# A cross-attention block on one core: one operand of the MLP made elsewhere, x scaled by another engine, and sums and stores reordered

## The chip, the cores and the metric

One core of a Trainium2 chip runs one program. The metric is the time of one execution in microseconds (us), as the device reports it; lower is better. Engines are named as in the profile: PE (TensorE, matmuls and transposes), DVE (VectorE), ACT (ScalarE), POOL (GpSimd) and SP (SyncE, which here does nothing but issue DMAs). Each engine runs its own instructions in the order in which the kernel emits them, and waits for the others by semaphores.

## What is computed

A cross-attention layer with an MLP in float32. `x` and `ctx` have 8 batches of 256 tokens of width 512 each. Cut to what matters:

```python
x = layer_norm(hidden_states, ln1_w, ln1_b)
q = x @ q_w + q_b                      # 512 x 512, 16 heads of 32
k, v = ctx @ k_w + k_b, ctx @ v_w + v_b
attn = softmax(where(mask, q @ k.T / sqrt(32), lowest))
hidden = (attn @ v) @ cproj_w + cproj_b + hidden_states
y = layer_norm(hidden, ln2_w, ln2_b)
y = gelu(y @ fc_w + fc_b)              # 512 -> 2048
return hidden + y @ proj_w + proj_b    # 2048 -> 512
```

## The kernel before

**Tiling.** The 2048 rows of tokens are worked on in 4 groups of 512 (`NG = 4`, `G = 512`), each two batches of 256. A tile has 128 partitions. First comes the attention of all four groups, then the MLP of all four.

**Strassen products.** Every 512-wide matrix product is made of seven products of quarters instead of eight, after Strassen and Winograd. Each needs sums and differences of the quarters of both operands: `A_SUMS` for a weight (s3 = 11 - 21, s2 = 22 - s3, 21 = s2 + 11, s4 = 12 - s2), `B_SUMS` for the tokens. An operand therefore has seven blocks: four quarters, one of them overwritten, and three sums. These sums run on POOL and DVE beside PE. In the attention's projections `strassen` (L417) emits the seven products as pieces p0 to p6.

**The attention's order is written by hand.** A group has 8 units (`u`), two per head group. The loop at L1040 emits, for unit n: the scores of unit n+2, softmax pieces of n+2 (DVE takes the maximum, ACT the exponential), the transposes of unit n's probabilities (`turn_probs`, L688, four per unit, PSUM tag "pt" with two buffers), the division of unit n+1 (`divide`, L676, four operations on POOL), and `attend` (L700), whose result is copied from a "pt" buffer to the tile `att` by ACT at L716. Between these steps other work is hung in: `between[g, u, 0..1]` holds PE's pieces of the next group's projections, `aside[g, u, 0..3]` holds sums, loads and stores. `begin(g, u, i, f)` appends to `aside[g, u, i]`; `spread` does so for a list. So a place such as (0, 6, 1) reads: group 0, unit 6, second stop.

**Layer norm of x.** `layer_norm` (L236) returns three kinds of pieces: statistics on DVE, the roots on POOL (L250 and L251), and the scaling of a 128 x 512 tile (L254) on a given engine. In the attention `norm_over` (L770) hangs these into units 2 to 4 for group g+2's x, with POOL as the engine of the scaling. The transposes of x (`turn_x`, L397, PE at L267) follow in units 5 and 6.

**The lent buffer.** The MLP's weight `fc_w` is also needed as Strassen sums. They are made during the attention and kept in DRAM (`w2_dram`). In group 0 this uses a place of the weights, `fc["a"]`, and a buffer lent by the attention: `fc["b"]`, which lies in the tile "att" that group 1 will need (L996). `sums` and `split` (L895 and L900) put each sum at its place; `keep_s3`, `keep_own` and `keep_first_s2` store results on SP. Before L716 may write group 1's first `att`, everything that reads the lent buffer has to be done, its stores included.

**The end of the attention.** `project_out(3)` (L618) projects the last group; its results are added on POOL to the residual `res` (L623) and stored from there to `hid_dram` (L624). `bias_res(3)` (L613, L616) adds a bias to one quarter of the residual on POOL and is emitted before the products 21, 22 and 12 of the projection. After the stores comes `load_w2("c")` (L1077).

**The MLP.** For each group `product(k, ...)` (L1232) makes the seven products of `fc_w`'s operands with the tokens, and `FC_ORDER` gives each its operand. An operand `w2[g, k]` occupies one of the places "q", "k", "c" and "v", and the end of a product loads another operand into the place that it frees (L1292). Within a product there are seven parts on PE: `sub(1)`, `sub(6)`, `sub(7)`, `sub(5)`, and then a second part into banks 1, 7 and 5. ACT copies bank 1 to u1 (L1270) after the first part, and the second part into bank 1 accumulates after that copy. DVE makes u2 and u3 and moves results to one of four slots of `h["s3"]`, from which POOL adds them to `h` (`made`, L1254). When an `h` is complete, `gelu` queues eight ACTIVATEs (L1214), which `some_gelus` lets out between ACT's copies, in program order.

Product 6 of group 0 is a special case: its operand, quarter 22 of `fc_w`, is loaded raw after product 3 (into place "q"), its four sums run on POOL after product 4's adds (L1307 and L1308), and the sums are stored for the later groups (L1309).

After the products the second Strassen product follows, with `proj_w` in `pw` (seven tiles of 128 x 8 x 256: four quarters and t1, t2, t4). Its sums of `pw` are made in group 0 by DVE, 16 pieces let out by `some_pw` (L1316 and on): in order 12, t2, t1, t4. Its sums of `h` run on POOL (`sum_h`: s3, s2, s1, s4).

Of the kernel before, what the change touches and what calls it, by code (L numbers as in the profile page):

```python
# [10 lines left out]
F32 = mybir.dt.float32  # L11
U8 = mybir.dt.uint8
AF = mybir.ActivationFunctionType
# [3 lines left out]
P = 128  # L17
# [5 lines left out]
def tile_xattn_block(  # L23
# [164 lines left out]
    def load_w2(at):  # L188

        if not w2_order:  # L190
            return
        g, k = w2_order.pop(0)
        t = rows_of(place(f"w2_{g}_{k}", at).t)
        n = FC_ORDER[k][0]
        if (g, k) == (0, 6):
            load_fc_quarter(lambda i: t[:, i], n)
        elif n in OWN:
            load_fc_quarter(lambda i: t[:, i], n, (0, 1, 3))
            nc.sync.dma_start(t[:, 2], w2_dram[QI[n]][:, 2])
            nc.sync.dma_start(t[:, 4:7], w2_dram[QI[n]][:, 4:7])  # L200
        else:
            nc.sync.dma_start(t, w2_dram[QI[n]])
        w2[g, k], w2_place[g, k] = t, at
# [32 lines left out]
    def layer_norm(tiles, tag, eng=nc.vector):  # L236


        mv = small.tile([P, NT, 2], F32, tag="mv", name=f"mv_{tag}")
        rstd = small.tile([P, NT], F32, tag="rstd", name=f"rstd_{tag}")  # L240
        layer_norm.last = mv, rstd

        def stats(t):
            st = small.tile([P, nc.vector.BN_STATS_DIM], F32, tag="st", name=f"st_{tag}_{t}")
            nc.vector.bn_stats(st, tiles[t])
            nc.vector.bn_aggr(mv[:, t, :], st)

        def roots():
            ve = small.tile([P, NT], F32, tag="ve", name=f"ve_{tag}")
            nc.gpsimd.tensor_scalar_add(ve, mv[:, :, 1], EPS)  # L250
            nc.gpsimd.tensor_tensor(rstd, ve, neg_half, ALU.pow)  # L251

        def normalise(t):
            eng.tensor_scalar(  # L254
                tiles[t], tiles[t], mv[:, t, 0:1], rstd[:, t : t + 1], ALU.subtract, ALU.mult
            )

        return (
            [lambda t=t: stats(t) for t in range(NT)],
            roots,  # L260
            [lambda t=t: normalise(t) for t in range(NT)],
        )

# [52 lines left out]
    with ExitStack() as att:  # L316
# [422 lines left out]
        def begin(g, u, i, f, *args):  # L739
            aside[g, u, i].append(lambda: f(*args))  # L740
# [26 lines left out]
            for c in range(NC):  # L767
                nc.sync.dma_start(chunk(att_in[g], c), halves(att_dram[:, c, :]))

        def norm_over(g, tiles, of_, tag, places, eng=nc.gpsimd):  # L770

            begin(g, *places[0], start_norm, of_, tiles, tag, eng)
            parts = [(0, t) for t in range(NT)] + [(1, None)] + [(2, t) for t in range(NT)]
# [19 lines left out]
        for g in range(NG - 1):  # L793

            work_of = [project_qk(g + 1, "qT"), project_qk(g + 1, "kT"), project_v(g + 1)]
            ns = ((1, 2),) * 5 + ((1, 1),) * 3
            if g == 1:
                work_of.append(project_out(0))
                ns = (1, 2), (1, 2), (2, 2), (2, 2), (2, 2), (1, 2), (2, 2), (1, 2)
            tt = turn_ctx(g + 1)  # L800
            between[g, 0, 1] += tt[:2]
            between[g, 1, 1] += tt[2:]
            if g + 2 < NG:
                tx = turn_x(g + 2)
                between[g, 5, 1] += tx[:2]
                between[g, 6, 1] += tx[2:]
                sums_at(xnT, g + 2, [(g, 6, 2), (g, 7, 1), (g, 7, 1), (g, 7, 2)])
                begin(g, 1, 3, load_ctx, g + 2)
                begin(g, 0, 3, load_x, g + 2)
                norm_over(  # L810
                    g, xs, g + 2, "a", [(2, 1), (2, 1), (2, 2), (2, 2), (2, 2), (3, 1), (3, 2), (4, 1), (4, 2)]
                )
            share(g, sum(work_of, []), [(u, i, n) for u in range(UG) for i, n in enumerate(ns[u])])
            begin(g, 0, 3, load_mask, g + 1)
            begin(g, 5, 1, make_mask, g + 1)
            begin(g, 4, 3, load_qk, g + 1, 0)
# [88 lines left out]
        begin(0, 0, 3, fc_first)  # L905

        sums("b", "a", "b", ALU.subtract, (0, 2, 1), (0, 2, 1), (0, 2, 2), (0, 2, 2))
        split("a", (0, 0, 3, 1), (1, 0, 3, 2), (2, 0, 4, 1), (3, 0, 4, 2))
        begin(0, 4, 3, keep_own, "a", "11")
        split("b", (0, 0, 5, 1), (1, 0, 5, 2), (3, 0, 6, 1))  # L910
        begin(0, 5, 1, fc_load, "a", "22")

        sums("a", "a", "b", ALU.subtract, (0, 6, 1), (0, 6, 2), (0, 6, 2), (0, 7, 1))
        split("b", (2, 0, 7, 2))
        begin(0, 7, 3, keep_s3)
        begin(0, 7, 3, keep_first_s2)
# [17 lines left out]
        def first_w2():  # L934
            load_w2("q")
            w2[w2_order.pop(0)] = rows_of(fc["f"].t)
            w2_place[0, 1] = "k"

        begin(NG - 1, 1, 0, first_w2)
# [140 lines left out]
    with ExitStack() as mlp:  # L1080
# [54 lines left out]
        for g in range(NG):  # L1135
# [32 lines left out]

            norm = []

            def norm_next():

                seen, roots, _ = layer_norm(hids[g + 1], f"m{g + 1}")
                mv, rstd = layer_norm.last
                nm = small.tile([P, NT], F32, tag="nm", name=f"nm_{g + 1}")

                def shift():
                    nc.vector.scalar_tensor_tensor(nm, mv[:, :, 0], -1.0, rstd, ALU.mult, ALU.mult)

                norm.extend([*seen, roots, shift])  # L1180
                return nm, rstd

            def norm_piece():
                if g + 1 < NG:
                    if not norm_of:
                        norm_of.append(norm_next())
                    norm.pop(0)()

            norm_of = []

            def normalise_next():
                if g + 1 < NG:
                    nm, rstd = norm_of[0]
                    for t, xt in enumerate(hids[g + 1]):
                        nc.scalar.activation(
                            xt, xt, AF.Identity, bias=nm[:, t : t + 1], scale=rstd[:, t : t + 1]
                        )

            def bias_ht():

# [27 lines left out]
            def product(k, *sums):  # L1228


                wt, yn = w2[g, k], QI[FC_ORDER[k][1]]
                bank = {}  # L1232

                def y_of(n):
# [4 lines left out]
                def sub(n, w, b, first, last):  # L1239
                    if first:  # L1240
                        bank[n] = bank_of(n, f"pf{n}_{k}").rearrange("p i (j s) -> p (i j) s", j=2)
                    for m in range(HF // 2):
                        mm(
                            bank[n][:, m, :],
                            wt[:, QI[w], ts(m, P)],
                            y_of(b),
                            first and m == 0,
                            last,
                        )
# [198 lines left out]
```

## Time and profile before

| | us |
|---|---|
| median of 3 runs | 738.78 (738.63 to 739.22) |
| the profiled execution, as the device reports it | 738.66 |
| its span, first to last instruction | 736.6 |
| PE busy | 722.6 |
| POOL busy | 518.2 |
| DVE busy | 419.3 |
| ACT busy | 316.7 |
| PE standing for x (L254 on POOL), group 0, from 104.50 | 2.73 |
| PE standing for a "pt" buffer (L716 on ACT), from 140.21 | 1.28 |
| PE standing for product 6's sums (L221 on POOL), from 391.79 | 1.53 |
| PE standing for s3 (L1101 on POOL), four times, from 405.85 | 3.05 |

The span is 2.1 us less than the device's time, since the device's time has what lies before the first and after the last instruction. The granted clock of PE is 0.998 throughout. The attention takes the first 353 us of the span, the MLP's first group the next 100, and each further one 94. A busy PE is not a PE at its peak, but an idle one has certainly lost time: of the 736.6 us some 14 are without a matmul, the start and the end among them.

A line of the waits reads "engine line <- engine tile line: us in total, times, longest". A line of the timeline reads "start, duration, engine, line, operation, out<-in, shapes, count [idle before <-releaser]"; operations that follow one another are merged. `w`, `hs`, `h`, `pw` are tiles with their numbers left out.

### The profile page before, as it was taken

Reading aid. Unit: us, or ns where it says so; the run is one execution under the profiler, and the core shown is the slowest. Engines: PE = TensorE matmul, PEld = TensorE weight load, DVE = VectorE, ACT = ScalarE, POOL = GpSimd, SP = SyncE. Lnnn points to the kernel's source line nnn. Section 1 sums busy time; section 2 is a strip of 40 time slices with the busy share of each in tenths; the row PEclk is TensorE's granted clock in tenths of the full one; section 3 lists DMA queues with packets and bytes.
Section 4 is the critical chain, followed back from the end, with each engine's and each line's share of the span. In section 5 each row is a group of like instructions: output and inputs, shape, how many; then the busy total and the mean of one; then the engine's idle time right before and its main releaser. Section 6 shows DMA issues by size and latency. Waiting matters only on the chain.

```text
span 736.6 us, 14041 instructions
## 1 busy us (share of the span) xinstructions
PE 722.6 (98%) x5109; PEld 628.6 (85%) x5109; DVE 419.3 (57%) x1054; ACT 316.7 (43%) x896; POOL 518.2 (70%) x459
## 2 busy tenths in 40 slices
PE   9999989999999999999999899999999999999998
PEld 8888767777887777777998689998899988999986
DVE  3676745574557556888586585681156811566211
ACT  2276777765867787771123400226002160030500
POOL 3857899978686999997569960489504896047870
PEclk9999999999999999999999999999999999999999
DMA  9517524795348789652799601992018930172001
GB/s 297 193 59 226 194 102 158 248 331 178 92 139 279 270 276 311 203 160 86 286 397 379 252 0 58 386 327 103 0 58 340 338 138 0 58 263 96 1 0 58
DMA packets 73940, 135.16 MB, mean 183 GB/s; under 512 B 6756, under 2 KB 44944, under 8 KB 71184
## 3 DMA queue, kind: packets, MB, share of 16 engines
q1 hardware_dynamic: 73616, 134.24, 52.1%
q8 instruction: 41, 0.67, 0.4%
q14 instruction: 27, 0.22, 0.1%
q0 software_dynamic: 256, 0.02, 0.0%
HBM read 100.69 MB, written 33.55 MB: 182 GB/s over the span
## 4 chain that ended last, share of the span: by engine, by line
PE 85%; POOL 9%; issue 2%; DVE 2%; ACT 1%; DMA 0%; SPq 0%; POOLq 0%; DVEq 0%; ACTq 0%
PE py L1098 25%; PE pf L1098 22%; PE ppt L692 6%; PE po L434 6%; PE pqT L434 6%; PE pv L434 5%; PE s L639 4%; PE av L708 3%; PE pkT L434 3%; POOL pr L681 3%; PE pkT L531 2%; POOL h L1101 1%; PE pyt L267 1%; PE pxt L267 1%; POOL w_a L221 1%
## 5 line engine op out<-in xcount | busy, mean ns | idle before, releaser
L1101 POOL TENSOR_TENSOR h<-h,hs 128x512 f32<-128x512 f32 x100 | 126.7, 1292 | 121.2 <-DVE hs L1101 120.8
L1098 PE MATMUL pf<-y,w 128*128 128x128 f32 x1512 | 169.9, 275 | 1.5 <-POOL w L221 1.5
L1098 PEld LDWEIGHTS pf<-y,w 128*128 128x128 f32 x1512 | 169.6, 192 | 1.9 <-POOL w L221 1.7
L681 POOL TENSOR_TENSOR pr<-pr,rsum 128x512 f32<-128x512 f32 x128 | 129.7, 1045 | 32.4 <-DVE rsum L679 18.6
L667 ACT ACTIVATE pr<-pr,nmax 128x256 f32<-128x256 f32 x256 | 127.7, 502 | 36.7 <-DVE nmax L657 36.6
L657 DVE CUSTOM_DVE_ANT_0 pr<-s,mb 128x256 f32<-128x256 f32 x256 | 93.5, 413 | 45.5 <-PE s L639 39.4
L1270 ACT COPY u<-pf 128x512 f32<-128x512 f32 x28 | 16.4, 585 | 200.0 <-PE pf L1098 200.0
L1098 PE MATMUL py<-pw,h 128*128 128x256 f32 x384 | 84.9, 379 | 0.0
L1098 PE MATMUL py<-pw_t,h 128*128 128x256 f32 x384 | 84.2, 379 | 0.0
L1098 PEld LDWEIGHTS py<-pw_t,h 128*128 128x128 f32 x384 | 72.7, 190 | 9.8
L1098 PEld LDWEIGHTS py<-pw,h 128*128 128x128 f32 x384 | 72.4, 190 | 9.6
L692 PEld LDWEIGHTS ppt<-ident,pr 128*128 128x128 f32 x512 | 57.2, 140 | 16.4 <-issue 7.3
L692 PE MATMUL ppt<-ident,pr 128*128 128x128 f32 x512 | 69.0, 277 | 1.4 <-ACT att L716 1.3
L1101 DVE TENSOR_TENSOR resm<-py,resm 128x512 f32<-128x512 f32 (+1 forms) x21 | 13.6, 664 | 94.7 <-PE py L1098 85.0
L1214 ACT ACTIVATE h<-h,cols 128x256 f32<-128x256 f32 x128 | 52.0, 494 | 15.9 <-POOL h L1101 15.9
L1101 DVE TENSOR_TENSOR hs<-pf,u 128x512 f32<-128x512 f32 x72 | 49.5, 689 | 13.3 <-PE pf L1098 12.3
L1101 DVE TENSOR_TENSOR u<-pf,u 128x512 f32<-128x512 f32 x56 | 38.7, 691 | 30.4 <-PE pf L1098 26.4
L697 ACT COPY pt<-ppt 128x512 f32<-128x512 f32 x96 | 51.7, 573 | 7.3 <-PE ppt L692 7.3
L434 PE MATMUL pv<-vw,ctxT 128*128 128x256 f32 x224 | 53.7, 387 | 0.0
L434 PE MATMUL pqT<-xnT,qw 128*128 128x256 f32 x224 | 51.0, 379 | 0.0
L667 ACT ACTIVATION_READ_ACCUMULATOR pr<-pr,nmax 128x1 f32 x256 | 48.8, 190 | 0.0
L434 PEld LDWEIGHTS pv<-vw,ctxT 128*128 128x128 f32 x224 | 41.7, 193 | 5.7 <-issue 0.3
(145 smaller groups left out, 1068.9 us busy)
## 6 DMA issues: line engine op xcount, KB each, us to landing
w<-w_dram SPq DMA_DIRECT2D x16, 1792.0 KB, 8.6
w<-in_L_xattn_fc_w_dram SPq DMA_DIRECT2D x34, 256.0 KB, 5.8
w<-w_dram SPq DMA_DIRECT2D x10, 768.0 KB, 7.3
ctx<-in_ctx_dram SPq DMA_DIRECT2D x16, 256.0 KB, 5.1
x<-in_x_dram SPq DMA_DIRECT2D x16, 256.0 KB, 5.3
v_dram<-st_v SPq DMA_DIRECT2D x16, 256.0 KB, 2.3
v<-v_dram SPq DMA_DIRECT2D x16, 256.0 KB, 4.2
resx<-in_x_dram SPq DMA_DIRECT2D x16, 256.0 KB, 4.3
```

Source lines behind the costliest of these rows:

```text
L434: nc.tensor.matmul(bank[n][:, i, :], l[:, c, ts(i, P)], r[:, c, :], start=first and i == 0 and c == 0, stop=last and c == HC - 1, skip_gro ...
L639: nc.tensor.matmul(banks[j][:, i, :], qT[j * HD : (j + 1) * HD, b * S + i * P : b * S + (i + 1) * P], kT[j * HD : (j + 1) * HD, b * SK : ( ...
L657: nc.vector.tensor_tensor_reduce(pr[:, j, i, :], banks[j][:, i, :], mbias[g][1][:, b, :], scale=-SCALE, scalar=FLT_MAX, op0=ALU.add, op1=A ...
L667: nc.scalar.activation(pr[:, j, i, :], pr[:, j, i, :], AF.Exp, bias=nmax[:, j, i : i + 1], scale=-1.0, accum_out=sums[:, j, i : i + 1],)
L681: nc.gpsimd.tensor_tensor(pr[:, j], pr[:, j], rsum[:, j, :, None].to_broadcast([P, NQ, SK]), ALU.mult,)
L692: nc.tensor.transpose(ps[:, kc, ts(i, P)], probs[n][:, j, i, ts(kc, P)], ident)
L697: nc.scalar.copy(pt, ps)
L708: nc.tensor.matmul(av[j * HD : (j + 1) * HD, :], vs[g, hg][:, b * NK + kc, ts(j, HD)], pts[n, j][:, kc, :], start=(kc == 0), stop=(kc == N ...
L1098: nc.tensor.matmul(ps, lhsT, rhs, start=first, stop=last, skip_group_check=True)
L1101: eng.tensor_tensor(to, a, b, op)
L1214: nc.scalar.activation(h[n][:, :, p, :], h[n][:, :, p, :], AF.Gelu_apprx_tanh, bias=col(c_fcb, half * HF + p), scale=1.0,)
L1270: nc.scalar.copy(u1, bank[1])
```

## The change

1. **x on ACT.** `norm_over` takes ACT as its engine. `layer_norm` then makes nm = -mean * rstd in one small DVE operation (`shift`) and scales with an ACTIVATE (Identity, with bias nm and scale rstd). The pieces are ten instead of nine: the shift stands at (3, 2), the four scalings at (4, 1), (4, 1), (4, 2), (4, 2). This holds for the x of groups 2 and 3, in units of groups 0 and 1. The norms of the MLP, which already were of this form, now use the same function.
2. **Lent buffer.** The splits and sums of `fc["a"]` and `fc["b"]` take other places, most of them half a unit to a unit earlier, and so do `keep_own`, `fc_load`, `keep_s3` and `keep_first_s2`.
3. **Operand left to the MLP.** Quarter 22 for product 6 of group 0 is loaded at the start of the MLP into memory of `pw["t4"]` (four blocks) and `pw["t1"]` (three), right behind `load_w2("c")` on SP. Its four sums are emitted right behind product 0, ahead of product 1's adds on POOL, and its four stores on SP follow them, ahead of the loads of the next group's hidden states and of all operands that product 1 and later ones load. (0, 6) leaves the order of `load_w2`, so product 3 loads (1, 0) and so on; product 6 loads nothing.
4. **`some_pw`.** Four of the eight pieces of DVE after product 6 move behind the first add of the second product.
5. **Residual bias last.** `bias_res(3)` is emitted after the projection's last pieces.

```diff
@@ load_w2
-        if (g, k) == (0, 6):
-            load_fc_quarter(lambda i: t[:, i], n)
-        elif n in OWN:
+        if n in OWN:
@@ layer_norm
+        nm = small.tile([P, NT], F32, tag="nm", name=f"nm_{tag}") if eng is nc.scalar else None
...
+        def shift():
+            nc.vector.scalar_tensor_tensor(nm, mv[:, :, 0], -1.0, rstd, ALU.mult, ALU.mult)
+
         def normalise(t):
-            eng.tensor_scalar(
-                tiles[t], tiles[t], mv[:, t, 0:1], rstd[:, t : t + 1], ALU.subtract, ALU.mult
-            )
+            if eng is nc.scalar:
+                eng.activation(
+                    tiles[t], tiles[t], AF.Identity, bias=nm[:, t : t + 1], scale=rstd[:, t : t + 1]
+                )
+            else:
+                eng.tensor_scalar(
+                    tiles[t], tiles[t], mv[:, t, 0:1], rstd[:, t : t + 1], ALU.subtract, ALU.mult
+                )
...
-            roots,
+            (roots, shift) if eng is nc.scalar else roots,
@@ norm_over and its places
-        def norm_over(g, tiles, of_, tag, places, eng=nc.gpsimd):
+        def norm_over(g, tiles, of_, tag, places, eng=nc.scalar):
...
-                    g, xs, g + 2, "a", [(2, 1), (2, 1), (2, 2), (2, 2), (2, 2), (3, 1), (3, 2), (4, 1), (4, 2)]
+                    g, xs, g + 2, "a",
+                    [(2, 1), (2, 1), (2, 2), (2, 2), (2, 2), (3, 2), (4, 1), (4, 1), (4, 2), (4, 2)],
@@ the lent buffer
         sums("b", "a", "b", ALU.subtract, (0, 2, 1), (0, 2, 1), (0, 2, 2), (0, 2, 2))
-        split("a", (0, 0, 3, 1), (1, 0, 3, 2), (2, 0, 4, 1), (3, 0, 4, 2))
-        begin(0, 4, 3, keep_own, "a", "11")
-        split("b", (0, 0, 5, 1), (1, 0, 5, 2), (3, 0, 6, 1))
-        begin(0, 5, 1, fc_load, "a", "22")
-
-        sums("a", "a", "b", ALU.subtract, (0, 6, 1), (0, 6, 2), (0, 6, 2), (0, 7, 1))
-        split("b", (2, 0, 7, 2))
-        begin(0, 7, 3, keep_s3)
-        begin(0, 7, 3, keep_first_s2)
+        split("a", (0, 0, 3, 1), (1, 0, 3, 2), (2, 0, 3, 2), (3, 0, 4, 1))
+        begin(0, 4, 2, keep_own, "a", "11")
+        split("b", (0, 0, 4, 2), (1, 0, 5, 1), (3, 0, 5, 2))
+        begin(0, 4, 3, fc_load, "a", "22")
+
+        sums("a", "a", "b", ALU.subtract, (0, 6, 2), (0, 6, 2), (0, 6, 1), (0, 7, 1))
+        split("b", (2, 0, 6, 1))
+        begin(0, 6, 2, keep_s3)
+        begin(0, 7, 2, keep_first_s2)
@@ first_w2
             w2[w2_order.pop(0)] = rows_of(fc["f"].t)
+            w2_order.remove((0, 6))
@@ the end of the attention
+        run(o[4:])
         bias_res(3)
-        run(o[4:])
         run(later)
         load_w2("c")
@@ the start of the MLP
         pw_sums = sum_pw()
+        left = [
+            pw[n].rearrange("p c n -> p (c n)")[:, ts(i, HC * S)]
+            for n, k in (("t4", 4), ("t1", 3))
+            for i in range(k)
+        ]
+        load_fc_quarter(lambda i: left[i], "22")
@@ product
-                wt, yn = w2[g, k], QI[FC_ORDER[k][1]]
+                wt, yn = w2_of(g, k), QI[FC_ORDER[k][1]]
...
-                load_w2(w2_place[g, k])
+                if (g, k) in w2_place:
+                    load_w2(w2_place[g, k])
@@ the products of a group
             product(0, ("21", None))
+            if g == 0:
+                for to, a, b, op in A_SUMS:
+                    add(GP, left[QI[to]], left[QI[a]], left[QI[b]], op)
+                nc.sync.dma_start(w2_dram[QI["22"]][:, 2], left[2])
+                for i in range(4, 7):
+                    nc.sync.dma_start(w2_dram[QI["22"]][:, i], left[i])
             load_next()
             product(1, ("11", "21"))
...
                 load_pw("21")
-                last = Operand(w2[0, 6].rearrange("p i (h s) -> p i h s", h=HC))
-                sum_up(GP, last, A_SUMS, 0, 1, 2, 3)
-                keep_sums("22", w2[0, 6])
...
-            some_pw(8)
+            some_pw(4)
...
             turn_next(0)
             turn_next(1)
+            some_pw(4)
             proj(bank[1], "12", "21", False, True)
```

More of the change, by code (lines that the diff above doesn't have):

```diff
@@ L240, in layer_norm @@
         rstd = small.tile([P, NT], F32, tag="rstd", name=f"rstd_{tag}")
-        layer_norm.last = mv, rstd
+        nm = small.tile([P, NT], F32, tag="nm", name=f"nm_{tag}") if eng is nc.scalar else None
         def stats(t):
@@ L768, in reload_att @@
                 nc.sync.dma_start(chunk(att_in[g], c), halves(att_dram[:, c, :]))
-        def norm_over(g, tiles, of_, tag, places, eng=nc.gpsimd):
+        def norm_over(g, tiles, of_, tag, places, eng=nc.scalar):
             begin(g, *places[0], start_norm, of_, tiles, tag, eng)
-            parts = [(0, t) for t in range(NT)] + [(1, None)] + [(2, t) for t in range(NT)]
+            roots = [(1, 0), (1, 1)] if eng is nc.scalar else [(1, None)]
+            parts = [(0, t) for t in range(NT)] + roots + [(2, t) for t in range(NT)]
             spread(g, places, [lambda i=i, t=t: norm_part(tag, i, t) for i, t in parts])
@@ L1169, in tile_xattn_block @@
             norm = []
[L1171 to L1181, printed above, removed]
             def norm_piece():
                 if g + 1 < NG:
[L1185 to L1189, printed above, removed]
+                    if not norm:
+                        norm.append(layer_norm(hids[g + 1], f"m{g + 1}", nc.scalar))
+                        seen, roots, _ = norm[0]
+                        norm.extend([*seen, *roots])
+                    norm.pop(1)()
             def normalise_next():
                 if g + 1 < NG:
[L1193 to L1197, printed above, removed]
+                    for f in norm[0][2]:
+                        f()
             def bias_ht():
@@ L1244, in sub @@
                             bank[n][:, m, :],
-                            wt[:, QI[w], ts(m, P)],
+                            wt(w)[:, ts(m, P)],
                             y_of(b),
@@ L1291, in product, with w2_of @@
                 made("12", 5, u2)
-                load_w2(w2_place[g, k])
-            product(0, ("21", None))
+                if (g, k) in w2_place:
+                    load_w2(w2_place[g, k])
+            def w2_of(g, k):
+                if (g, k) != (0, 6):
+                    return lambda w: w2[g, k][:, QI[w]]
+                return lambda w: left[QI[w]]
+            product(0, ("21", None))
+            if g == 0:
[4 more added lines that the diff above has]
+                    nc.sync.dma_start(w2_dram[QI["22"]][:, i], left[i])
             load_next()
```

## The prediction

> **What bounds the kernel now.** I read the page first: which engine has no air.
>
> ```profile
> PE 722.6 (98%) x5109; PEld 628.6 (85%) x5109; DVE 419.3 (57%) x1054; ACT 316.7 (43%) x896; POOL 518.2 (70%) x459
> ...
> PE   9999989999999999999999899999999999999998
> DMA  9517524795348789652799601992018930172001
> ```
>
> TensorE is the bound, and the change takes no matmul away. So it can win only the places where PE stands still, and lose only by making new ones. PE does not fill the sixth and the 23rd slice (and the last, the kernel's end). In the slices around the 21st to 23rd the DMA engines are full too, which will count below. Second view, the waits of PE (in all, times, longest):
>
> ```profile
> PE py L1098 <- POOL hs L1101: 3.0, 4, 1.4
> PE pxt L267 <- POOL x L254: 2.7, 1, 2.7
> PE pf L1098 <- POOL w L221: 1.5, 1, 1.5
> PE ppt L692 <- ACT att L716: 1.3, 1, 1.3
> ```
>
> From the instruction records these gaps are 3.05, 2.73, 1.53 and 1.28 us, 8.59 us together; what else PE waits for is its start (1.4) and crumbs (0.2). The change aims at all four. The fourth is a DMA's: L716 itself waited for a store, as the waits of ScalarE say.
>
> ```profile
> ACT att L716 <- DMA w_dram<-w_b: 2.5, 1, 2.5
> ```
>
> Third view, the timeline of POOL (start, duration): four operations of x at 2.08 us sit in a full queue, four sums `w<-w` sit between the adds of products 4 and 5 of the MLP, and the sums `hs` (s3) come late behind them.
>
> ```profile
> 91.17 2.10 POOL L254 TENSOR_SCALAR x<-x,mv_a,rstd_a 128x512 f32<-128x512 f32 x1
> ...
> 105.09 2.08 POOL L254 TENSOR_SCALAR x<-x,mv_a,rstd_a 128x512 f32<-128x512 f32 x1
> ...
> 390.66 5.18 POOL L221 TENSOR_TENSOR w<-w 128x512 f32<-128x512 f32 x4
> ...
> 405.49 6.74 POOL L1101 TENSOR_TENSOR hs<-h,h 128x512 f32<-128x512 f32 x4
> ```
>
> Fourth, PE's own timeline in the MLP of group 0: 232 matmul records in 26.07 us, so a product (56) takes 6.29 us; products 3, 4, 5 and 6 begin at 372.0, 378.3, 384.6 and 390.9.
>
> ```profile
> 365.72 26.07 PE L1098 MATMUL pf<-y,w 128*128 128x128 f32 x232
> 393.32 5.62 PE L1098 MATMUL pf<-y,w 128*128 128x128 f32 x48 [1.52 <-POOL w L221]
> ```
>
> **x on ScalarE.** Four POOL operations of 2.08 us (8.3 us) leave group 0's attention and four leave group 1's; eight ACTIVATEs come, for which L1195 has the same form: 0.80 us each, one every 0.70. In group 0 all four x are ready by about 101 us, before the transposes at 104.0, so the 2.73 us go. What is late next: in unit 4 ScalarE runs, in this order, two copies to 96.47, x0 and x1 (to 97.87), two exponentials (to 98.87), the copy of pv (to 99.36), x2 and x3 (to 100.77), then L716 to 101.14, where it ended at 100.01. The second transpose of the next unit needs the bank that L716 frees; PE would reach it at 101.0 and resumes 0.14 after L716 (as at 141.49 after 141.35): 0.3 us lost. In group 1 the same shift ends L716 at 183.9, before PE asks at 184.2: nothing. The added VectorE operation on 128x4 (L1178: 0.69 to 1.23 us) is a unit ahead of its use. Net **-2.43**.
>
> [...]
>
> **The lent buffer.** Its sums are the same count on POOL, placed earlier into the room that x leaves. `keep_s3` (five stores, issued from 131.80 to 138.93 now) moves up one unit, behind a sum that POOL now does there instead of in unit 7, and the last reader of the buffer, the fourth sum of "a", ends at 133.2 (135.60 less the 2.43 won before); L716 wants the buffer at 136.1 (138.54 less 2.43). The 1.28 us go: **-1.28**. The divides keep their lead: POOL's work of unit 6 (115.64 to 127.91) exchanges one sum for another and moves with PE, so the next divide's first tile is again done 0.5 before PE asks (128.90 and 129.41 now).
>
> **The operand in proj_w's places.** What goes: product 6 no longer waits for POOL (-1.53), and without 5.18 us of sums ahead the s3 sums are in time (-3.05). What comes must be followed through SP, whose timeline is:
>
> ```profile
> 353.06 2.91 SPq L624 DMA_DIRECT2D hid_dram<-resx  x3
> 356.02 3.98 SPq L202 DMA_DIRECT2D w<-w_dram  x2
> 360.09 1.98 SPq L229 DMA_DIRECT2D hm<-hid_dram  x4
> 365.92 0.32 SPq L202 DMA_DIRECT2D w<-w_dram  x1
> ```
>
> SP issues in order. With the bias last on POOL, the last hid store waits for one more add (1.27), so the load for product 2 is issued at 357.25 instead of 356.02; it took 7.40 and lands at 364.7, needed at 365.7: covered, with 1 us left. Then come the four loads of the operand (256 KB each). The rows land in the order of issue (hm at 369.78, 370.44, 371.12, 371.79, after product 3's operand at 369.09), 0.67 us apiece: the operand is there at 367.4, its third block at 366.7. POOL sums it from 366.7 to 371.8 (5.1). Queued behind these sums on POOL are product 1's three adds, which ran at 364.0 to 368.3: now 371.8 to 375.6. For the last of these waits ScalarE's gelu:
>
> ```profile
> 366.81 0.58 ACT L1270 COPY u<-pf 128x512 f32<-128x512 f32 x1 [5.67 <-PE pf L1098]
> 367.42 1.28 ACT L1214 ACT_TABLE_LOAD   x1
> 368.71 3.30 ACT L1214 ACTIVATE h<-h,cols 128x256 f32<-128x256 f32 x8
> 373.07 0.59 ACT L1270 COPY u<-pf 128x512 f32<-128x512 f32 x1 [1.05 <-PE pf L1098]
> ```
>
> The eight gelus run 375.6 to 378.9, and behind them stands the copy of product 3's first bank, 378.9 to 379.5 instead of 373.07. PE must not accumulate into that bank before. After four of product 3's seven parts (0.90 each) it is there at 375.6 and **waits 3.9 us**; the three last parts then follow VectorE's u2, u3 and made (0.70 each), and product 3 ends at 382.85 instead of 378.3: **+4.55**.
>
> The DMAs say nearly the same on their own. Ahead of product 4's operand now stand the late issue (1.24), the four loads (2.69, as 383.24 to 385.93) and the four stores (2.49 for the same bytes, 402.19 to 404.68), and the engines are full:
>
> ```profile
> 357.50:378.30 20.80, 20.80 (x189) 20.80 (x188) 13.56 (x22) 6.93 (x13) 8.82 (x7) 1.00 0.99 398
> ```
>
> (the last two columns are DMA share and GB/s). It landed at 376.1 and lands at 381.2 to 382.5, wanted at 378.3. So even if ScalarE's chain were shorter, 2.9 us stay. Product 5's operand (383.24) comes at 388.7 to 389.7, wanted at 389.1: +0.3. Product 6 ends near 402.1 instead of 398.9, s3 begins 6.9 later; POOL's s3 sums at 1.68 apiece beside VectorE's sums of proj_w (405.5, 407.2, 408.8, 410.5) hold its last quarter: +0.4. Together **+5.25** against -4.58. The four sums of proj_w that move behind the projection's first add are wanted only at 425: nothing. The refactoring of the later norms issues the same instructions.
>
> **Bounds.** Two prices are not in the trace. The landing of the operand: 364.7 if it flows beside the load ahead of it (then the 2.9 of the DMAs stays), 373.1 if it shares the engines with the load behind (5.67 more, one for one through the chain: 10.9 in all). I take the queue's order, which the hm rows show. ScalarE's four x: 0 if its idle time takes them, 1.1 (the whole delay of L716) if PE has no slack; I take 0.3.
>
> **Sum.** 738.66 - 2.43 - 1.28 - 4.58 + 5.25 = 735.62 us by the profiled execution (span 736.6), which is 0.12 under the median: 735.6.
>
> **Rivals.** *All four waits go and nothing comes*: 738.66 - 8.59 = 730.1. For it: POOL idles from 356.3 to 364.0. Against: the operand can't land before 364.7, and SP and POOL are in order. *Half of it*, if the gelus' chain is shorter and only DMA counts: 5.25 - 1.65, 734.0, and down to 732 if its loads overlap better. *Slower*: the operand lands with product 3's operand at 373.1, because one engine's share of a transfer lags; 2 KB packets of hm did run before product 3's operand had landed. Then the chain restarts PE 5.7 us later, 741.3; from a landing at 369.1 on there is no gain that can be measured, from 372.1 on it is slower. *No change*: L716 or the divides take the place of both waits in the attention, 3.7 us back: 739.3; against it, ScalarE has 2.6 us of idle time between 90.4 and 99.5 for the 2.8 that x takes.
>
> **How the numbers follow.** A measurement can tell about 0.2%, 1.5 us, from none: faster is below 737.3, slower above 740.3. The forecast (733.5 to 737.3) gets 0.60, all four waits gone 0.10, between them 0.08, no change 0.12, slower 0.10. The range of 730.1 to 739.5 leaves the slower case out. Faster 0.78, same 0.12, slower 0.10.
>
> **What would show it.** Right: no wait of PE for POOL x, POOL w or `hs` beyond 0.5 us; one new gap of 3 to 5 us inside product 3 of group 0, put down to ScalarE's copy of u or a load of w; POOL's four sums near 367 to 372, product 1's adds behind them. Wrong: sums that begin before 362, a gap above 6 us there, or PE waiting for L716, exponentials or divides in units 4 to 8 for more than 1 us.

## The result: 742.16 us, slower, and the profile after

The changed kernel takes **742.16 us** (median of 5, 741.66 to 743.30) where the kernel before takes 738.98 in the same series (738.63 to 739.22): ratio 1.0045, 95% interval 1.0030 to 1.0059. The forecast was 735.6 with a range of 730.1 to 739.5, and the time lies outside it. The profiled execution of the changed kernel is the longest of its five, 743.30 (span 741.1); 1.05 us of that is a stand in unit 24, described at the end, which not every profiled execution shows.

The page of the changed kernel, its first and second part (busy time, then the span in 40 slices):

```profile
PE 723.8 (98%) x5109; PEld 630.4 (85%) x5109; DVE 417.9 (56%) x1056; ACT 321.8 (43%) x904; POOL 501.6 (68%) x451
...
PE   9999999799999999999979999999999999999998
```

POOL lost 16.6 us of work and ACT took 5.1, as announced. But the hole in PE has not been closed, it has moved: the sixth slice is full now, the eighth (129.7 to 148.2 us) has one, and the hole of the 23rd slice (where s3 waited) is gone, and a new one stands in the 21st (370.6 to 389.1). PE's busy time even rose by 1.2 us, with the same 5109 instructions. The waits of PE in the changed kernel (in all, times, longest):

```profile
PE av L715 <- DMA v<-v_dram: 5.2, 2, 4.2
PE pf L1108 <- ACT u L1274: 3.5, 1, 3.5
PE pf L1108 <- DMA w<-w_dram: 1.9, 2, 1.3
...
PE pf L1108 <- DVE u L1111: 0.4, 1, 0.4
PE pf L1108 <- DVE hs L1111: 0.4, 1, 0.4
...
PE py L1108 <- POOL hs L1111: 0.3, 1, 0.3
```

The four waits that the change aimed at are gone (of s3's 3.05 us 0.3 is left). The second to fifth rows are the forecast gap in product 3 and its neighbours (the loads of w: 1.28 in front of product 3 and 0.67 in front of product 5). **The first row was not foreseen at all**: PE stands 4.17 us, from 133.41, for the load of v that is issued in unit 7 of group 0; the attend behind it is that of unit 8 (units are counted on over the groups here: unit 8 is the first of group 1). In two stretches that can be cut out of both traces (from the attend of unit 4 to that of unit 9, and from the MLP's first matmul to the second product's first one behind the eight transposes of the next tokens, 417.58 before and 422.26 after), with PE's gaps added up:

| stretch | before: length = gaps + rest | after | forecast | measured |
|---|---|---|---|---|
| units 4 to 9 | 50.59 = 4.01 + 46.58 | 50.81 = 4.26 + 46.55 | -3.71 | +0.22 |
| MLP of group 0 | 64.36 = 4.57 + 59.79 | 68.07 = 6.45 + 61.62 | +0.67 | +3.71 |

The two spans differ by 4.55; the 0.62 that the table leaves are the stand in unit 24 (1.05) less crumbs.

**Where the load of v is late** is read on SP. Its timeline in the changed kernel (start, duration):

```profile
117.64 1.59 SPq L889 DMA_DIRECT2D w_dram<-w_b  x3
119.28 0.64 SPq L890 DMA_DIRECT2D w_dram<-w_b_sums  x1
121.61 2.90 SPq L494 DMA_DIRECT2D v_dram<-st_v  x2
131.39 0.33 SPq L885 DMA_DIRECT2D s_dram<-w_a  x1
131.83 0.37 SPq L587 DMA_DIRECT2D v<-v_dram  x1
```

`keep_s3` (L889, L890) comes out early, as predicted. Then SP issues nothing from 124.5 to 131.39 (6.8 us of this the waits of SP put down to POOL's line L907): the next instruction in its order is the store of `keep_first_s2` (L885), and it waits for POOL's fourth sum of "a":

```profile
SPq L885 <- POOL w_a L907: 6.8, 1, 6.8
```

The load of v (L587) stands behind it. The chain that ended last, in order of time, goes through exactly these steps:

```profile
130.10 1.27 POOL w_a L907
131.38 0.02 issue
131.39 0.33 SPq L885
...
131.83 5.62 DMA v<-v_dram
137.44 0.14 issue
137.58 1.60 PE av L715 x16
```

In the kernel before the load of v was issued at 130.36, the store at 139.42, in the other order. The diff moves `keep_first_s2` from (0, 7, 3), where the loads of v and of q and k had been hung in before it, to (0, 7, 2), ahead of them.

**The MLP.** The waits of SP over the whole span hold a longer row of the same kind:

```profile
SPq L1309 <- POOL pw_t L1111: 12.1, 1, 12.1
```

SP stands 12.1 us at the first store of the left operand's sums. Behind it are the loads of the next hidden states, of product 4's operand (issued at 377.80) and of product 5's (378.75). POOL's and ACT's timelines show the chain that the prediction followed:

```profile
369.62 1.27 POOL L1111 TENSOR_TENSOR pw_t<-pw_t 128x512 f32<-128x512 f32 x1 [11.07 <-PE pf L1108]
370.96 3.83 POOL L1111 TENSOR_TENSOR pw_t<-pw_t,pw_t 128x512 f32<-128x512 f32 x3
374.75 7.40 POOL L1111 TENSOR_TENSOR h<-h,hs 128x512 f32<-128x512 f32 x6
```

```profile
378.51 3.30 ACT L1218 ACTIVATE h<-h,cols 128x256 f32<-128x256 f32 x8 [8.83 <-POOL h L1111]
381.72 0.56 ACT L1274 COPY u<-pf 128x512 f32<-128x512 f32 x1
```

Product 1's adds stand behind the sums, the gelus behind the adds, the copy of product 3's first bank behind the gelus, 2.8 us later than worked out (0.97 of it is the MLP's later start).

**A term that isn't in the waits.** Behind the gaps of 4.17 and 3.48 us the granted clock is 0.50, for 3.41 us each. Stretches of the changed kernel (bounds, length, busy time of PE, PEld, DVE, ACT and POOL with counts, then granted clock, DMA share, GB/s):

```profile
137.99:141.40 3.41, 3.41 (x32) 1.76 (x23) 0.08 (x1) 0.47 (x1) 0.65 (x1) 0.50 1.06 391
141.40:145.00 3.60, 3.60 (x27) 3.34 (x27) 3.60 (x16) 3.21 (x12) 2.02 (x3) 1.00 1.12 331
383.75:387.16 3.41, 3.31 (x15) 3.31 (x16) 3.24 (x7) 0.00 (x0) 1.56 (x2) 0.50 0.95 375
387.30:393.00 5.70, 5.70 (x54) 5.70 (x53) 4.00 (x8) 0.58 (x1) 3.14 (x3) 1.00 1.02 406
```

In the third stretch 15 matmul records take 3.31 us of PE, in the fourth 54 take 5.70: 0.22 and 0.11 us each. The kernel before has one such stretch too, one us behind the gap for x (so the 0.998 given above for that kernel is a mean, not its clock throughout):

```profile
108.25:111.66 3.41, 3.41 (x15) 2.06 (x17) 0.00 (x0) 1.37 (x3) 3.41 (x4) 0.50 0.59 194
```

Where this gap is gone, the attend of unit 5 comes 3.97 us sooner behind that of unit 4 (12.56 before, 8.59 after). So a gap of 2.73 us cost about 4 us; the rows of the waits show only the gap.

### The profile page after: what moved, and what is told of

Read it like the earlier page. It is cut to its first block, busy times and chain, and to the rows that moved or that the text cites. A ratio compares the mean times of both kernels' runs of the same rounds, so it can differ in the third digit from the quotient of the medians.

```text
span 741.1 us, 14045 instructions
## 1 busy us (share of the span) xinstructions
PE 723.8 (98%) x5109; PEld 630.4 (85%) x5109; DVE 417.9 (56%) x1056; ACT 321.8 (43%) x904; POOL 501.6 (68%) x451
## 4 chain that ended last, share of the span: by engine, by line
PE 90%; POOL 4%; DMA 3%; issue 2%; DVE 1%; ACT 0%; SPq 0%; POOLq 0%; DVEq 0%
PE py L1108 25%; PE pf L1108 22%; PE ppt L699 7%; PE pqT L441 6%; PE po L441 6%; PE pv L441 6%; PE pkT L441 5%; PE s L646 5%; PE av L715 4%; DMA w<-w_dram 2%; PE pkT L538 2%; DMA v<-v_dram 1%; POOL pr L688 1%; PE pxt L274 1%; PE pyt L274 1%
## 5 line engine op out<-in xcount | busy, mean ns | idle before, releaser
L1108 PE MATMUL pf<-y,w 128*128 128x128 f32 x1456 | 166.3, 277 | 6.1 <-ACT u L1274 3.5
L1108 PEld LDWEIGHTS pf<-y,w 128*128 128x128 f32 x1456 | 165.2, 193 | 7.3 <-ACT u L1274 3.7
L441 PEld LDWEIGHTS pqT<-xnT,qw 128*128 128x128 f32 x224 | 41.4, 190 | 5.0
```

Source lines behind the costliest of these rows:

```text
L441: nc.tensor.matmul(bank[n][:, i, :], l[:, c, ts(i, P)], r[:, c, :], start=first and i == 0 and c == 0, stop=last and c == HC - 1, skip_gro ...
L1108: nc.tensor.matmul(ps, lhsT, rhs, start=first, stop=last, skip_group_check=True)
```

## The experiments

All ratios are to the kernel before, run on the same chip in the same series.

**1. The store of the first s2 back behind the loads.** One line:

```diff
-        begin(0, 7, 2, keep_first_s2)
+        begin(0, 7, 3, keep_first_s2)
```

> The changed kernel with one line undone: the store of the first s2 (four blocks of the weight a) goes back from the third to the last stop of group 0's unit 7, behind the loads of v, kT and qT on SP. Theory (SP's order): in the changed kernel this store waits on SP for POOL's fourth sum of a (131.37), and the load of v for the next unit, 131.83 to 137.44, stands behind it. Undone, v is issued near 126.7 and lands before PE asks at 133.4: the 4.17 us wait goes, and with it the 3.41 us at half clock that followed (1.5 us), so 742.16 - 5.7 = 736.5. Rival (the DMA engines are the limit: the lent buffer's five stores, 1.8 MB, now run in unit 6): v still lands after 135.5 and at most 2 us are won, 740 or more.

Measured: 736.62 (735.64 to 737.65), ratio 0.9960 [0.9944, 0.9976]. SP's timeline in this kernel:

```profile
127.16 0.36 SPq L587 DMA_DIRECT2D v<-v_dram  x1
127.61 0.46 SPq L582 DMA_DIRECT2D kT<-kT_dram  x1
128.12 0.70 SPq L582 DMA_DIRECT2D qT<-qT_dram  x1
131.85 0.32 SPq L885 DMA_DIRECT2D s_dram<-w_a  x1
```

The wait for v and the half clock behind it are gone (the clock of 137.99 to 141.40 is 1.00); units 4 to 9 take 45.01 = 0.09 + 44.92. One line on SP decides between slower and faster than before.

**2. The left operand undone** (loaded after product 3, summed after product 4, as before; the rest of the change stays):

```diff
+        if (g, k) == (0, 6):
+            load_fc_quarter(lambda i: t[:, i], n)
...
-        load_fc_quarter(lambda i: left[i], "22")
...
-                for to, a, b, op in A_SUMS:
-                    add(GP, left[QI[to]], left[QI[a]], left[QI[b]], op)
...
+                sum_up(GP, last, A_SUMS, 0, 1, 2, 3)
+                keep_sums("22", w2[0, 6])
```

> The changed kernel with the operand of product 6 handled as before (loaded after product 3, summed and stored after product 4's adds); x on ACT, the lent buffer, the late bias and the split of proj_w's sums stay. By the two traces product 6 ended 7.2 us later against the start of the MLP and 3.5 us of that came back at s3. So the operand's part costs 3.7 us: 742.16 - 3.7 = 738.5, and the waits for POOL's w (1.5) and hs (up to 3.0) are there again, the wait for ACT's u (3.5) and the second stretch at half clock are not. Rival (the late bias delays everything alike and the operand is not the cause): a wait of over 1 us for a load of w stays, and less than 1.5 us is won.

Measured: 740.31 (738.85 to 741.41, 10 runs), ratio 1.0008 [0.9999, 1.0017]. The waits of product 6 and of s3 are back at 1.54 and 3.05, and from the MLP's first matmul to the second product's first it is 45.58 where the kernel before has 45.56. So the operand costs some 2.7 us net in the ratios (expected 3.7), and the two edits that stay, the late bias and the split of the sums of `pw`, cost or win nothing there. Of the missing 1 us the profiled execution shows 0.95 in the attention: units 4 to 9 take 51.76 where the changed kernel takes 50.81, and the half clock behind v lasts 6.83 us instead of 3.41.

**3. Both undone.** The edits of 1 and 2 together.

> Both of the two edits above undone: what remains is x on ACT, the lent buffer's sums and stores (but for the one store), the late bias and the split of proj_w's sums. If the two costs are separate stages, as the trace says, they add: 742.16 - 5.7 - 3.7 = 732.8, and that beats the kernel before by 6 us: 4.0 for the wait for x with its stretch at half clock, 1.3 for the wait for att, and up to 1 for s3 beside four sums of proj_w instead of eight. Rival (the waits trade places, PE stands for divides or exponentials of group 0 instead): 736 or more.

Measured: 734.40 (733.65 to 734.56), ratio 0.9928 [0.9911, 0.9944], where 732.8 was expected. The two costs, as experiments 1 and 2 measured them, add. What is left of the change in this kernel, x on ACT and the reordered sums, wins 0.7%, more than the 3.71 us that the prediction gave it.

**4. PE kept at work in product 3's gap**, with 24 transposes into a bank that nobody reads (extra work, no part of the result):

```diff
+                if (g, k) == (0, 3):
+                    idle = ps_m.tile([P, G], F32, tag="mm", name="idle")
+                    for t in range(24):
+                        nc.tensor.transpose(idle[:, ts(t % NT, P)], ident, ident)
                 sub(1, "12", "21", False, True)
```

> The changed kernel with 24 transposes of the identity into an unused bank, in product 3 of group 0 where PE stands 3.48 us for ACT's copy of u; nobody reads them, and they add 2.7 to 3.2 us of work for PE within the wait. The trace shows a granted clock of 0.5 from 383.75 to 387.16, right behind that wait, and none behind the four short waits of the kernel before. Theory (standing still is what halves the clock): the wait for the copy ends at the same time, the stretch at half clock is gone, 1.5 to 1.7 us won: 740.6. [...] Rival (the half clock comes from load or chance, or the added work itself delays PE): 742 to 744.

Measured: 743.06 (742.30 to 743.31), ratio 1.0045 [1.0030, 1.0060]: nothing won, where 740.6 was expected. The half clock in the MLP did go (the only stretch at 0.5 is now that behind v; the mean clock is 0.998, where the changed kernel has 0.995). But PE's timeline shows what stood behind it:

```profile
377.68 2.78 PE L1288 MATMUL idle<-ident 128*128 128x128 f32 x24
381.32 1.16 PE L1108 MATMUL pf<-y,w 128*128 128x128 f32 x8 [0.86 <-ACT u L1274]
382.85 2.05 PE L1108 MATMUL pf<-y,w 128*128 128x128 f32 x16 [0.36 <-DVE u L1111]
386.48 6.52 PE L1108 MATMUL pf<-y,w 128*128 128x128 f32 x56 [1.58 <-DMA w<-w_dram]
394.03 2.16 PE L1108 MATMUL pf<-y,w 128*128 128x128 f32 x17 [1.04 <-DMA w<-w_dram]
```

Product 4 begins as late as in the changed kernel (33.1 us after the MLP's first matmul in both): here PE waits 1.58 us for its operand, which had not landed. ACT's copy and SP's late load are two bounds, one just behind the other.

**5. The sums and stores behind product 1**, so that product 1's adds go first on POOL:

```diff
+            load_next()
+            product(1, ("11", "21"))
             if g == 0:
                 for to, a, b, op in A_SUMS:
...
-            load_next()
-            product(1, ("11", "21"))
```

> The changed kernel with the four POOL sums of the left operand and their four stores emitted behind product 1 (so product 1's adds go first on POOL, and the loads of the next hidden states and of product 4's operand go ahead of the stores on SP). Theory (the loss in the MLP is one of order on POOL and SP): product 1's adds end near 369 instead of 378.5, so ScalarE's copy for product 3 isn't late: the wait of 3.48 us, the two small ones of 0.35 and the half clock behind them (some 1.5) go; product 4's operand is issued some 5 us earlier and lands near 381.4 where PE wants it at 380.7, so 0.7 to 1.7 us of waiting for it appear; the wait of 1.28 for product 3's operand stays. Some 4 us less: 738, ratio to before 0.999. Rival (the DMA engines are so full that product 4's operand lands at 385 or later, whatever the order): PE waits there for 4 us or more in place of ScalarE, 741.5 to 742.

Measured: 741.88 (740.23 to 743.35, 10 runs), ratio 1.0034 [1.0025, 1.0044]. The expected 738 fell. Its steps held up to product 4: ACT's wait is gone, product 4's operand lands at 380.39 and PE waits 0.47 for it. The next link did not:

```profile
373.45 6.52 PE L1108 MATMUL pf<-y,w 128*128 128x128 f32 x56 [1.36 <-DMA w<-w_dram]
380.44 6.52 PE L1108 MATMUL pf<-y,w 128*128 128x128 f32 x56 [0.47 <-DMA w<-w_dram]
390.31 5.95 PE L1108 MATMUL pf<-y,w 128*128 128x128 f32 x38 [3.35 <-DMA w<-w_dram]
```

Product 5's operand is now the one that stands behind the stores. It is issued at 375.51 and lands at 390.26, and behind its 3.35 us comes a half clock again (0.73 on the mean of 387.30 to 393.00). A third bound had been hidden by the first two.

**6. Only the stores moved**, behind the load of quarter 21 of `proj_w`:

```diff
-                nc.sync.dma_start(w2_dram[QI["22"]][:, 2], left[2])
-                for i in range(4, 7):
-                    nc.sync.dma_start(w2_dram[QI["22"]][:, i], left[i])
...
                 load_pw("21")
+                nc.sync.dma_start(w2_dram[QI["22"]][:, 2], left[2])
+                for i in range(4, 7):
+                    nc.sync.dma_start(w2_dram[QI["22"]][:, i], left[i])
```

> The changed kernel with only the four stores of the left operand's sums moved on SP, behind the load of the quarter 21 of proj_w after product 4; the sums stay ahead of product 1's adds on POOL. Theory (two chains stand one behind the other, ScalarE's copy and SP's late load): ScalarE's wait of 3.5 us in product 3 stays with its half clock, product 4's operand is issued near 370 to 372 and lands near 381.4, long before PE asks at 387; only the wait for product 5's operand (0.67) goes: 741.5 to 742.2. Rival (the late load of product 4's operand is what the MLP pays for): 739 or less.

Measured: 742.44 (742.15 to 743.48), ratio 1.0046 [1.0032, 1.0061]. ACT's 3.48 us and their half clock stay; the operands of products 4 and 5 land at 381.83 and 388.81, and PE waits for neither. Alone, SP's part of the loss is worth nothing that can be measured.

**7. Both moved**, the edits of 5 and 6:

> The changed kernel with the left operand's sums on POOL behind product 1's adds and, besides, its stores behind the load of quarter 21 of proj_w. Theory (three chains one behind another: ScalarE's copy, product 4's operand, product 5's operand; the order on POOL is to blame for the first, the stores on SP for the two others): what stays is 1.3 us for product 3's operand, 0.5 for product 4's and 0.3 for product 5's (it landed 34.1 us after the start of the MLP with the stores late, and was wanted 33.8 after it without ScalarE's wait), and no half clock in the MLP: 5.5 us under the changed kernel, 736.6, ratio 0.997. Rival (the operand's 1.8 MB fill the DMA engines wherever the stores are): product 5's operand is again 2 us or more late with a half clock behind it, 739 or more.

Measured: 736.88 (736.06 to 737.25), ratio 0.9962 [0.9949, 0.9975].

```profile
374.83 6.52 PE L1108 MATMUL pf<-y,w 128*128 128x128 f32 x56 [2.02 <-DMA w<-w_dram]
381.85 6.52 PE L1108 MATMUL pf<-y,w 128*128 128x128 f32 x56 [0.50 <-DMA w<-w_dram]
388.77 6.52 PE L1108 MATMUL pf<-y,w 128*128 128x128 f32 x56 [0.40 <-DMA w<-w_dram]
```

Two edits of which one wins 0.1% at most (within the intervals) and the other nothing win 0.8% together (1.0045 to 0.9962). PE's 2.02 us of waiting in front of product 3 are 0.7 more than expected; no half clock follows.

**8. x back on POOL**, on the kernel of experiment 1:

```diff
-        def norm_over(g, tiles, of_, tag, places, eng=nc.scalar):
+        def norm_over(g, tiles, of_, tag, places, eng=nc.gpsimd):
...
-                    [(2, 1), (2, 1), (2, 2), (2, 2), (2, 2), (3, 2), (4, 1), (4, 1), (4, 2), (4, 2)],
+                    [(2, 1), (2, 1), (2, 2), (2, 2), (2, 2), (3, 1), (3, 2), (4, 1), (4, 2)],
```

> The changed kernel with the store of the first s2 behind the loads again (736.6 so far), and with x scaled on POOL at its old places. Theory (x on POOL alone costs PE the stand in unit 5, and the half clock behind it): a wait of 2.7 us or more for L254 in unit 5 with 3.4 us of half clock behind it, 4 us in all: 740.6, ratio 1.002; the lent buffer's sums stand earlier on POOL now, so it may be more: up to 742. Rival (the other order of the lent buffer's sums is what freed POOL): no wait for x, 736.6.

Measured: 744.32 (742.49 to 745.23), ratio 1.0065 [1.0048, 1.0082], beyond the expected 740.6 to 742. PE waits twice for x, and the clock is halved behind it (108.48 to 111.90):

```profile
105.51 0.33 PE L274 MATMUL pxt<-ident,x 128*128 128x128 f32 x1 [0.58 <-POOL x L261]
108.79 1.33 PE L274 MATMUL pxt<-ident,x 128*128 128x128 f32 x5 [2.96 <-POOL x L261]
```

Units 4 to 9 take 50.57 where experiment 1's kernel takes 45.01. So 5.56 of the 7.7 us between the two medians lie here; of the rest, this profiled execution has 0.97 in unit 24's stand, and a half clock of 6.83 instead of 3.41 us in product 3. The reordered sums need the room that x left on POOL; without the move to ACT they would have made x later than before.

**9. The whole change, put together otherwise**: the line of experiment 1, the bias first again, the left operand loaded behind product 3's operand, its sums behind product 2's adds and its stores behind quarter 21 of `proj_w`. Besides, the loads of the next hidden states go behind product 1, and three quarters of `proj_w` are loaded ahead of product 3 instead of behind it; these two were not tried alone. Cut to what matters:

```diff
             product(0, ("21", None))
             if g == 0:
+                load_fc_quarter(lambda i: left[i], "22")
+            product(1, ("11", "21"))
+            load_next()
+            gelu("11", 0)
+            product(2, ("21", "21"))
+            if g == 0:
                 for to, a, b, op in A_SUMS:
                     add(GP, left[QI[to]], left[QI[a]], left[QI[b]], op)
+                load_pw("22", "12", "11")
+            ht = residual(work, hid_dram[g], "resm", f"resm_{g}")
+            product(3, ("12", "21"))
...
                 load_pw("21")
+                nc.sync.dma_start(w2_dram[QI["22"]][:, 2], left[2])
+                for i in range(4, 7):
+                    nc.sync.dma_start(w2_dram[QI["22"]][:, i], left[i])
```

> A kernel that keeps what won and moves what lost: the store of the first s2 behind the loads; the residual's bias ahead of the last products again; the left operand loaded on SP behind product 3's operand (after product 0) instead of ahead of everything, its sums on POOL behind product 2's adds, its stores behind the load of quarter 21 of proj_w. Theory: no wait in products 2 to 5, and the waits of product 6 (1.53) and of s3 (3.05) stay away, so it is 4 to 4.6 us under the kernel with both edits undone (734.4): 730, ratio 0.988. Rival (a further operand of 1.8 MB among full DMA engines makes some operand or quarter of proj_w late wherever it is put): 1 to 4 us of waits for a load in the products 3 to 6 or at the start of the second product, 731 to 734.4.

Measured: **727.91** (727.44 to 728.15), ratio **0.9845** [0.9831, 0.9860], 2 us better than expected. All that PE waits for in this kernel, by its waits:

```profile
PE warm L992 <- POOL ident masks.py:199: 1.4, 1, 1.4
PE py L1108 <- POOL hs L1111: 0.3, 1, 0.3
PE av L715 <- DMA v<-v_dram: 0.2, 1, 0.2
PE av L715 <- ACT pt L704: 0.2, 1, 0.2
```

The MLP's stretch of the table takes 59.03 = 0.30 + 58.73. On POOL the same four sums of 5.2 us now have nothing of product 1 behind them, and ACT's copy for product 3 runs at 368.02, right behind PE, where it was at 381.72:

```profile
367.14 2.51 POOL L1111 TENSOR_TENSOR h<-h,hs 128x512 f32<-128x512 f32 x2 [0.58 <-DVE hs L1111]
369.60 1.27 POOL L1111 TENSOR_TENSOR pw_t<-pw_t 128x512 f32<-128x512 f32 x1
370.95 3.85 POOL L1111 TENSOR_TENSOR pw_t<-pw_t,pw_t 128x512 f32<-128x512 f32 x3
374.77 9.90 POOL L1111 TENSOR_TENSOR h<-h,hs 128x512 f32<-128x512 f32 x8
```

**10 and 11. Two of its choices taken back**, each alone: the load of the left operand at the start of the MLP again, and the bias last again.

```diff
+        load_fc_quarter(lambda i: left[i], "22")
...
-            if g == 0:
-                load_fc_quarter(lambda i: left[i], "22")
             product(1, ("11", "21"))
```

> The best kernel so far with one line back: the left operand is loaded at the start of the MLP, ahead of product 3's operand, as in the change. Theory (with the bias first, product 3's operand has 3.3 us of air and the four loads take 2.7 of them): a wait of 0 to 0.3 us, 728. Rival (the place of the loads cost the 1.3 us of waiting for product 3's operand in the change): 729.3 or more.

```diff
-        bias_res(3)
         run(o[4:])
+        bias_res(3)
```

> The best kernel so far with the residual's bias last again, as in the change. Theory (all loads of the MLP start 1.2 us later, and each has more air than that when the left operand's loads stand behind product 3's operand): no new wait, 728. Rival (product 2's operand, which the late bias delays directly, or product 4's becomes late): 729 to 730.

Measured: 728.51 (727.75 to 730.08), ratio 0.9853 [0.9839, 0.9868], with 0.41 us of waiting for product 3's operand, and 728.12 (727.81 to 728.95), ratio 0.9848 [0.9831, 0.9864], with none. Neither place matters by itself: the air in front of product 3 takes one of the two delays. The kernels that have both (the changed one and experiments 1 and 4 to 8) wait there for 1.1 to 2.0 us.

## Why the prediction was wrong

**The step that failed** is that of the lent buffer: "`keep_s3` (five stores ...) moves up one unit ... The 1.28 us go: -1.28". The store `keep_first_s2` in the same hunk moves from (0, 7, 3) to (0, 7, 2), and that step was left out: I followed the lent buffer on POOL, through L716 and the divisions, and not through SP. There it passes the load of v and makes it wait for POOL (131.39), 4.17 us of standing and a half clock. Experiment 1 puts one line back and the ratio goes from 1.0045 to 0.9960, a difference of 6.3 us. This alone turned the sign. It was none of the rivals: they looked for the slower side in the MLP. With the line back the time, 736.62, is near the forecast, but by luck: two sizes were wrong and nearly cancel. Units 4 to 9 win 5.58 us (50.59 to 45.01) instead of 3.71, and the MLP's stretch loses 3.07 (64.36 to 67.43) instead of 0.67.

**x on ACT, -2.43.** Right in its mechanism, too small: the attend of unit 5 comes 3.97 us sooner after unit 4's (12.56 before, 8.59 after), and 2.43 were forecast. The missing term is the clock: behind the 2.73 us the transposes and matmuls of 108.25 to 111.66 ran at half of it. The 0.3 us charged for L716 was right: the eight transposes behind it take 1.38 us where they took 1.09 (the records overlap, so PE shows only 0.09 of it as idle). (One reading on the way was loose, and nothing rests on it: the DMA engines fill the 21st and 22nd slice, but six tenths of the 23rd.)

**Lent buffer, -1.28.** The wait for L716 goes in all kernels that have the new places; from the attend of unit 7 to that of unit 9 it is 21.65 before and 20.07 in experiment 1, -1.58.

**Operand, -4.58.** Right: product 6's 1.53 is gone and of s3's 3.05 only 0.3 is left.

**Operand, +5.25.** The chain (sums, product 1's adds, gelus, copy) was right link by link: 3.9 us forecast for PE's wait, 3.48 measured. That the two are so near is partly luck: the operand's third block landed at 369.46 instead of 366.7, and PE reached the bank 3.25 us later too (378.85 instead of 375.6), because the MLP began 0.97 later and product 3 waited 1.28. The size of the whole was wrong: 3.04 us more (+3.71 for +0.67). Of these, 1.20 are more gaps (6.45 for 5.25): by its own terms product 3's operand, behind the four loads, had to land about 373 (369.09, later by 1.24 and 2.69) and was wanted at 372.0, but I only asked when the left operand would land; it cost 1.28. And 1.83 are slower matmuls (61.62 for 59.79), most of it the half clock behind the gap: 15 records took 3.31 us there, which at 0.11 each are 1.6. The operand of product 4 was forecast for 381.2 to 382.5 and landed at 386.57: I added the bytes of the four stores and not the 12.1 us in which SP stands at the first of them. Experiments 4 to 7 show what that hides: ACT's copy, product 4's operand and product 5's lie so close behind one another that no single cure tried wins more than about 0.1%.

**Late bias and `some_pw`.** Nothing, as predicted (experiments 2 and 11), so long as no other delay takes the same air.

## What to carry to other kernels

A store whose data was not ready held up the loads behind it on SP, for 6.8 us at L885 and 12.1 us at L1309 of the changed kernel: for each store that a change moves or adds, list the loads it now stands ahead of and compare the time at which its producer ends with the time at which they have to be issued. Here these two stores and one order of sums and adds on POOL made most of the difference between +0.45% and -1.55% (experiments 1 and 7 add to 1.7 of the 2.0 points), with the same count of instructions on every computing engine. When a cure removes the longest wait and the time does not move, look for the next operand in line and cure both at once before the idea is dropped.

## What the runs showed of the hardware

**A gap in PE has a second price.** In the profiled executions of the kernel before and of the changed kernel the granted clock is 1.00 or 0.50, and between start and end a stretch at 0.50 lasts 3.41 us; experiments 2 and 8 have one of 6.83 us each. The clock fell at gaps of 2.73 to 4.21 us: 2.73 (the kernel before), 4.17 and 3.48 (the changed kernel), 4.21 (experiment 2), 4.21 and 3.35 (experiment 5), 2.96 and 3.48 (experiment 8). At the 2.02 us of experiment 7 it did not: the mean clock of that execution, 0.998, is that of one stretch in 735.5 us, and the line that makes v late stands in that kernel. In experiments 3, 9 and 10, where the longest gap is 1.5, 1.4 and 1.4 us, the mean clock is 1.00. What a gap between 2.02 and 2.73 us does, and why two stretches are twice as long, was not shown.

**A stand in unit 24 that comes and goes.** PE waits for the load of v there 1.05 us in the profiled execution of the changed kernel, 1.22 in experiment 10's, but 0.2 in experiment 9's and none in the kernel before or in experiments 1 and 11. The code of this unit is the same in all of them. What decides it was not tried and stays open; it may be part of the spread of 1 to 2 us between executions.
